# A macaron network on one core: first recurrence and mixer preparation, per sequence instead of per batch

## The chip, the core and the metric

The kernel runs on one core of a Trainium2 chip. A core has five engines that run side by side, each with its own queue, taken in order: TensorE (PE, matmuls and transposes, its weight loads listed as PEld), VectorE (DVE), ScalarE (ACT), GpSimd (POOL) and SyncE (SP, which here only issues transfers; ACT's queue issues a few as well). Matmul results land in PSUM, from where DVE and ACT fetch them. The metric is the device time of one execution in microseconds (us), lower is better; a matmul of 32-bit floats is two passes in the trace, each with a weight load.

## The reference, cut to what matters

Eight sequences of 512 tokens with 128 features go through four layers. Every layer is a half-weighted feed-forward part, a mixing part, and the same feed-forward part again, each on a layer-normed input and added to x. Only the first layer's first two parts are touched:

```python
def ffn(x, ...):                       # L0_ffn: a gated recurrence over the 8 SEQUENCES (the scan axis),
    def step(c, xt):                   # side by side for all 512 tokens
        ft = sigmoid(xt @ wf.T + c @ uf.T + bf)
        it = sigmoid(xt @ wi.T + c @ ui.T + bi)
        gt = tanh(xt @ wc.T + c @ uc.T + bc)
        return ft * c + it * gt, None
    c_final, _ = lax.scan(step, c0, x)
    return tanh(einsum('tbi,oi->tbo', x, wo) + c_final @ uo.T + bo)

def mixer(u, ...):                     # L0_attn: a state-space mixer along the tokens
    zxbcdt = u @ W_in.T                # z0, x0 (skip), xBC (conv), dt (8 heads)
    dt = softplus(dt + dt_bias); A = -exp(A_log)
    xBC = silu(causal_conv4(xBC) + conv_b)          # x, B, C
    h = exp(dt*A) * h + dt * x * B;  y = h . C + D * x        # step by step over the tokens
    y = layernorm(y) * ln_gamma + ln_beta
    y = sigmoid(y @ W_gate.T + b_gate) * y
    return concat([silu(z0) * x0, y]) @ W_out.T

x = x + 0.5 * ffn(layernorm(x)); x = x + mixer(layernorm(x)); x = x + 0.5 * ffn(layernorm(x)); ...
```

The outputs of the first part need c_final, so nothing of the mixer can begin before all eight steps of the recurrence are done.

## The kernel before

x stays on the chip all the way, one tile x0 to x7 per sequence (128 partitions, 4 chunks of 128 tokens, 128 features). The weights come in packs by one transfer each. The stages of the list `_STAGES` follow one another: l0_ffn, l0_attn, l0_ffn again, then the layers behind, which the diff does not touch. They take the span from about 495 us on.

The order in which Python emits the instructions is not quite the order on the engines. The framework's planner takes what is ready by its own estimate, earlier emitted first, when an engine is free; tiles with the same name in a pool share `bufs` buffers and are handed out in the order of emission. The result is a fixed order on each engine. The planner does not read the trace.

**l0_ffn** (L452) norms all sequences (`norm`, L331: statistics on DVE, power of -1/2 on POOL, application on DVE), turns them on PE to xT0 to xT7 (`transposed`, L434, copied from PSUM by ACT, L439), and runs the recurrence: for each sequence three gates, each a matmul with xT and one with c into a PSUM tile pf, pi or pc (L329 is the helper `mm`), an activation on ACT (L474), and on DVE fc, ig and the new c (L476 to L480). Behind the last step come the product of c with uo, the tile cb (L485), and for each sequence the product with wo, h (L491), its tanh (L492) and the half addition to x (`add_half`, L448).

**l0_attn** (L495) prepares the mixer for all eight sequences at once. `norms` (L360) takes four sequences together, with one power on POOL for 16 columns (L374), and applies on ACT (L381). After the first four, `mixer_in(0)` (L591) is emitted except its first piece: conv 2, 0, 1 (each a matmul, one ACT pass L609 and three DVE passes L612), skip 0 and 1 (L623, L624), silu (L630 to L633), and b_tokens (L660). Then for all 32 chunks together: 64 passes with w_dt, the softplus (L831 to L849, a power series in some 16 DVE instructions on 128x256, with one Exp on ACT), la = dt times the rates, three products with constant triangles (running sums), and from them cum, since_start, to_end and whole, kept in `self.tokens`.

The mixer's loop goes over the sequences; in a pass for b, pieces of five kinds are emitted by the slot numbers of `_MIXER`:

```python
_MIXER = dict(
    weights=(0, 4, 6, 12),
    sums=(9, 14, 21, 29),
    turned=(17, 23, 29, 35),
    inputs=(7, 19, 21, 23, 25, 27, 29, 31),
    out=(2, 6, 8, 10, 18, 22, 25),
)
```

`weights`, `sums` and `turned` are the four chunks of b (`chunk_weights` L675 with the Exp named decay, L702, read from the PSUM tile pr; `chunk_sums` L718 with brought and the state; `chunk_turned` L758); `inputs` is `mixer_in(b + 1)`, whose first piece, exponents, makes from cum the tiles from, to_rows and to (L646 to L652); `out` is `mixer_out(b - 1)` (L767: norm of y, turns, two sigmoid gates L804, product, addition to x L819). PSUM has three buffers of the name mm, three of ck, and one pr of two banks. The loop's pool sb has two buffers of a name unless it says otherwise.

A third way to norm stands further down and is used by later stages: `front` (L1175) gives two functions, stats (DVE statistics, POOL's power) and apply (an offset on DVE, four normalisations on ACT, L1200).

## Time and profile before

| | us |
|---|---|
| median of three runs | 2368.93 |
| the three runs | 2368.93, 2368.0, 2375.28 |
| span of the profiled execution (no time of its own is listed beside it) | 2372.5 |
| busy in the span: PE, DVE, ACT, POOL | 2109.1, 1631.6, 1269.6, 660.6 |
| c of the recurrence first multiplied, last c written | 27.6, 72.3 |
| first and second sequence's first decay | 151.45, 170.69 |
| mixer's last addition to x | 425.96 |
| TensorE clock granted, mean of the span | 0.937 |

A row of a group or of the timeline names the line, the engine, the operation and the tiles (out<-in). "[0.39 <-DVE c L466]" is the idle time of the engine before the instruction and what ended it. A row of busy times gives a stretch, its length, and the busy time of each engine in it with the number of instructions, then the granted TensorE clock (1.00 is full speed). The chain of waits is the chain of work that ended last, followed back from the end. Busy PE overlaps itself, since matmuls are pipelined.

### The profile page before, as it was taken

The page shows a single profiled execution, that of the slowest core. Times are in us where ns is not written, and L with a number is a line of the kernel's source. Part 1 is how long each engine was busy: PE and PEld are TensorE (multiplying, and loading weights), DVE is VectorE, ACT ScalarE, POOL GpSimd, SP SyncE. Part 2 cuts the span into 40 slices and gives each one's busy share as a digit, 9 for nine tenths or more (in the row PEclk, how much of TensorE's full clock was granted, in tenths as well). Part 3 has the DMA queues.
Part 4 walks back from the last instruction along what each step waited for, and adds up shares of the span by engine and source line. Part 5 has one row for each costly group of instructions (what it writes and reads, how often), then busy time and mean ns, then how long its engine had stood idle before and what let it go on. Part 6 is the DMA issues. An engine that isn't in the chain of part 4 may idle for free.

```text
span 2372.5 us, 30011 instructions
## 1 busy us (share of the span) xinstructions
PE 2109.1 (89%) x10967; PEld 1001.9 (42%) x10967; DVE 1631.6 (69%) x3830; ACT 1269.6 (54%) x1857; POOL 660.6 (28%) x923
## 2 busy tenths in 40 slices
PE   7679999979998888999996999896789999999989
PEld 3344444444433333333332444444445444444444
DVE  4556775368888788888827889888776556666611
ACT  3545665323322376777772446666674355555554
POOL 1124433013212011111113233446552123333330
PEclk9778998979999999999997999998897999999999
DMA  3000000000000000000000000000000000000001
GB/s 124 1 1 1 1 1 1 14 10 1 1 1 1 1 1 1 1 1 1 1 1 7 1 1 1 0 1 1 0 1 0 1 1 1 1 1 1 2 1 36
DMA packets 10035, 13.07 MB, mean 6 GB/s; under 512 B 416, under 2 KB 8736, under 8 KB 9760
## 3 DMA queue, kind: packets, MB, share of 16 engines
q1 hardware_dynamic: 7776, 10.11, 1.3%
q8 instruction: 86, 1.41, 0.3%
q10 hardware_dynamic: 2112, 1.05, 0.2%
q14 instruction: 61, 0.50, 0.1%
HBM read 9.06 MB, written 2.10 MB: 5 GB/s over the span
## 4 chain that ended last, share of the span: by engine, by line
PE 60%; DVE 23%; POOL 7%; ACT 7%; issue 3%; DMA 0%; ACTq 0%; DVEq 0%; SPq 0%; POOLq 0%
PE pair L329 11%; PE av L329 8%; PE mm L329 8%; PE po L329 6%; PE pu L329 5%; PE first L329 4%; DVE max L1673 4%; PE pg L329 3%; ACT e L1781 3%; PE ck L329 2%; PE pr L329 2%; DVE act L942 2%; PE big L329 1%; PE ph L329 1%; DVE xn L355 1%
## 5 line engine op out<-in xcount | busy, mean ns | idle before, releaser
L1673 DVE TENSOR_REDUCE max<-first 128x1 f32<-128x512 f32 (+3 forms) x756 | 468.3, 664 | 173.4 <-PE first L329 166.1
L1781 ACT ACTIVATE e<-pair 128x1024 f32<-128x1024 f32 (+3 forms) x512 | 436.5, 864 | 239.3 <-PE pair L329 227.1
L329 PE MATMUL first<-qkT 32*128 32x512 f32 (+3 forms) x896 | 267.9, 443 | 30.5 <-DVE max L1673 28.7
L329 PE MATMUL pair<-qkT 32*128 32x512 f32 (+3 forms) x1024 | 222.5, 454 | 20.0 <-ACT e L1781 14.6
L329 PE MATMUL av<-e,v 128*32 128x512 f32 (+3 forms) x2048 | 238.9, 536 | 0.1
L941 ACT ACTIVATE act<-pg 128x512 f32<-128x512 f32 x144 | 85.6, 596 | 212.9 <-PE po L329 122.0
L329 PEld LDWEIGHTS pair<-qkT 32*128 32x128 f32 x1024 | 95.2, 185 | 233.6 <-ACT e L1781 133.2
L329 PE MATMUL pair<-mT,max_rows 32*128 32x512 f32 (+3 forms) x1024 | 190.4, 374 | 1.7 <-DVE mT L1715 1.7
L329 PE MATMUL pu<-xT,w_moe 128*128 128x512 f32 x288 | 158.4, 632 | 18.8 <-DVE act L942 14.0
L1783 POOL TENSOR_SCALAR_AFFINE_SELECT e<-e 128x256 f32<-128x256 f32 x256 | 103.4, 407 | 253.4 <-ACT e L1781 253.1
L329 PE MATMUL po<-act,w_moe 128*128 128x512 f32 x288 | 161.3, 647 | 5.4 <-DVE act L949 4.2
L329 PE MATMUL pg<-xT,w_moe 128*128 128x512 f32 x288 | 150.5, 620 | 4.4 <-ACT act L941 3.3
L329 PEld LDWEIGHTS first<-qkT 32*128 32x128 f32 x896 | 119.6, 185 | 69.4 <-DVE max L1673 66.9
L942 DVE TENSOR_TENSOR act<-act,pu 128x512 f32<-128x512 f32 x144 | 97.8, 679 | 28.8 <-PE pu L329 23.5
L1679 POOL COPY copies<-max 128x128 f32<-128x128 f32 x64 | 23.6, 424 | 272.4 <-DVE max L1673 272.4
L329 PEld LDWEIGHTS pair<-mT,max_rows 32*128 32x128 f32 x1024 | 96.9, 188 | 3.0 <-DVE mT L1715 2.7
L1673 DVE TENSOR_REDUCE max<-mm 128x1 f32<-128x512 f32 (+3 forms) x108 | 70.9, 665 | 36.7 <-PE mm L329 35.5
L949 DVE TENSOR_TENSOR act<-act,big 128x512 f32<-128x512 f32 x128 | 86.3, 677 | 12.3 <-PE big L329 11.8
L329 PEld LDWEIGHTS pu<-xT,w_moe 128*128 128x128 f32 x288 | 50.2, 196 | 76.8 <-DVE act L942 37.0
L329 PEld LDWEIGHTS po<-act,w_moe 128*128 128x128 f32 x288 | 50.5, 199 | 63.5 <-issue 28.1
L978 POOL TENSOR_TENSOR ge<-ge,w_moe 128x64 f32<-128x64 f32 (+1 forms) x32 | 42.8, 1336 | 119.1 <-DVE ge L976 113.6
L329 PEld LDWEIGHTS pg<-xT,w_moe 128*128 128x128 f32 x288 | 51.1, 195 | 57.2 <-issue 40.1
(423 smaller groups left out, 4398.2 us busy)
## 6 DMA issues: line engine op xcount, KB each, us to landing
w_moe<-in_moe SPq DMA_DIRECT2D x1, 2392.0 KB, 14.0
out<-x SPq DMA_DIRECT2D x8, 256.0 KB, 2.3
x<-in_u ACTq DMA_DIRECT2D x4, 256.0 KB, 6.6
x<-in_u SPq DMA_DIRECT2D x4, 256.0 KB, 6.4
w_mixer<-in_l0a SPq DMA_DIRECT2D x1, 960.5 KB, 8.2
w_mixer<-in_l1a SPq DMA_DIRECT2D x1, 769.0 KB, 4.8
w_ffn<-in_l0f SPq DMA_DIRECT2D x1, 578.0 KB, 7.2
w_ffn<-in_l2f SPq DMA_DIRECT2D x1, 560.0 KB, 3.3
```

Of the source, the lines that this page charges most:

```text
L329: self.nc.tensor.matmul(out, lhsT, rhs, start=start, stop=stop)
L355: nc.vector.tensor_scalar(xn[:, c, :], x[:, c, :], mv[:, c, 0:1], rstd[:, c : c + 1], ALU.subtract, ALU.mult)
L941: nc.scalar.activation(act, pg, AF.Silu)
L942: nc.vector.tensor_tensor(act, act, pu, ALU.mult)
L949: nc.vector.tensor_tensor(act, act, pw[:, e % 2, :], ALU.mult)
L978: nc.gpsimd.tensor_tensor(ge.rearrange(flat), ge.rearrange(flat), self.wide(before, m), ALU.mult)
L1673: nc.vector.tensor_reduce(mx[:, c, j, gs[0] : gs[-1] + 1], sc, AX.X, ALU.max, negate=True)
L1679: nc.gpsimd.tensor_copy(copies[:, :, :, :, g], mx[:, :, :, g].unsqueeze(3).to_broadcast([P, NC, 4, 8]),)
L1781: nc.scalar.activation(e[:, :, :n], sc[:, :, :n], AF.Exp, scale=scale)
L1783: nc.gpsimd.affine_select(e[:, :, :P], e[:, :, :P], pattern=[[0, 2], [1, P]], compare_op=ALU.is_ge, fill=0.0, base=0, channel_multiplier=-1,)
```

## The change

The first l0_ffn leaves the list of stages; its recurrence moves into l0_attn as `l0_chain`, and its outputs go into a new list of six pieces per sequence, `mixer_ready`: out (product with wo, h, tanh, half addition), stats and apply (with `front`), turned, steps (w_dt, softplus, la) and sums (running sums and their exponentials). In `l0_chain` the norm and the turn of a sequence are emitted right before its own step of the recurrence, with statistics one sequence ahead. The pieces of sequences 0 and 1 are emitted ahead of the mixer's loop, mixed with `mixer_in(0)`; those of sequence b + 2 are emitted in the loop's pass for b, at the slots `ready`. What was one tile for all 32 chunks in `self.tokens` becomes a tile of 32 columns per sequence, with two buffers. The transfers at the start change their order: on SP x0, w_const, w_ffn, x2, x4, x6, then the other packs; on ACT x1, x3, x5, x7 as before.

```diff
@@ -222,6 +222,7 @@
     out=(2, 6, 8, 10, 18, 22, 25),
+    ready=(3, 5, 11, 13, 16, 24),
@@ -299,11 +300,19 @@
+        self.ident = None
+
+        def fetch(eng, b):
+            eng.dma_start(out=self.x[b], in_=u[b].rearrange("(c p) d -> p c d", p=P))
+
+        fetch(nc.sync, 0)
         self.load("const")
-        for b in range(NB):
-            eng = nc.sync if b % 2 == 0 else nc.scalar
-            eng.dma_start(out=self.x[b], in_=u[b].rearrange("(c p) d -> p c d", p=P))
-        for name in ("l0f", "l0a", "moe", "heads", "l2a", "l3f"):
+        for b in range(1, NB, 2):
+            fetch(nc.scalar, b)
+        self.load("l0f")
+        for b in range(2, NB, 2):
+            fetch(nc.sync, b)
+        for name in ("l0a", "moe", "heads", "l2a", "l3f"):
             self.load(name)
         self.ident = self.w["const", "ident"]
         self.nhalf = const.tile([P, 4 * NC], F32, name="nhalf")
@@ -492,82 +501,90 @@
+    def l0_chain(self, keep):
+
+
+        nc = self.nc
+        w = lambda n: self.w["l0f", n]
+        self.xT = [keep.tile([P, L], F32, name=f"xT{b}") for b in range(NB)]
+        self.last_c = keep.tile([P, L], F32, name="last_c")
+        with ExitStack() as s:
+            sb = s.enter_context(self.pool("sb", 2))
+            ps = s.enter_context(self.pool("ps", 2, space=bass.MemoryType.PSUM))
+            c = sb.tile([P, L], F32, name="c")
+            nc.vector.memset(c, 0.0)
+            nc.vector.tensor_scalar(c, c, w("in_c"), None, ALU.add)
+            fronts = [self.front(b, "i", 2, lambda: sb) for b in range(NB)]
+            for b in range(NB):
+                if b == 0:
+                    fronts[0][0]()
+                if b + 1 < NB:
+                    fronts[b + 1][0]()
+                fronts[b][1]()
+                self.transposed(fronts[b][2]["xn"], ps, self.xT[b], nc.scalar.copy)
+                gates = {}
+                for gate, func in (("f", AF.Sigmoid), ("i", AF.Sigmoid), ("c", AF.Tanh)):
+                    pg = ps.tile([P, L], F32, name=f"p{gate}")
+                    self.mm(pg, w("w" + gate), self.xT[b], stop=False)
+                    self.mm(pg, w("u" + gate), c, start=False)
+                    gates[gate] = sb.tile([P, L], F32, name=f"g{gate}")
+                    nc.scalar.activation(gates[gate], pg, func, bias=w("b" + gate))
+                fc = sb.tile([P, L], F32, name="fc")
+                nc.vector.tensor_tensor(fc, gates["f"], c, ALU.mult)
+                ig = sb.tile([P, L], F32, name="ig")
+                nc.vector.tensor_tensor(ig, gates["i"], gates["c"], ALU.mult)
+                c = sb.tile([P, L], F32, name="c") if b + 1 < NB else self.last_c
+                nc.vector.tensor_tensor(c, fc, ig, ALU.add)
+
     def l0_attn(self):
...
         with ExitStack() as s:
             keep = s.enter_context(self.pool("keep", 1))
+            self.l0_chain(keep)
             sb = s.enter_context(self.pool("sb", 2))
             ps = s.enter_context(self.pool("ps", 3, space=bass.MemoryType.PSUM))
             self.key, self.sb, self.ps = "l0a", sb, ps
-            for b in range(0, NB, 4):
-                for k, xn in enumerate(self.norms(range(b, b + 4), keep)):
-                    t = keep.tile([P, L], F32, name=f"xT{b + k}")
-                    xT.append(self.transposed(xn, ps, t, nc.scalar.copy))
-                if b == 0:
-                    self.seqs = [{"xT": xT[0]}]
-                    first = self.mixer_in(0)
-                    for piece in first[1:]:
-                        piece()
-            self.seqs += [{"xT": t} for t in xT[1:]]
-            pd = ps.tile([P, NB * NC, H], F32, name="mm")
...
-            nc.vector.tensor_tensor(v, pd, self.wide(w("dt_bias"), NB * NC), ALU.add)
-            dt = keep.tile([P, NB * NC, H], F32, name="dt")
-            self.softplus(dt.rearrange("p t h -> p (t h)"), v.rearrange("p t h -> p (t h)"), keep)
...
+            self.seqs = [{} for _ in range(NB)]
+            pc = ps.tile([P, NC, P], F32, name="mm")
+            for t in range(NC):
+                self.mm(pc[:, t, :], self.last_c[:, bass.ts(t, P)], self.w["l0f", "uo"])
+            self.cb = keep.tile([P, NC, P], F32, name="cb")
+            nc.vector.tensor_tensor(self.cb, pc, self.wide(self.w["l0f", "bo"]), ALU.add)
+            ready = [self.mixer_ready(b) for b in range(NB)]
+            a = self.rates = keep.tile([P, H], F32, name="a")
             nc.scalar.activation(a, w("A_log"), AF.Exp)
...
-            pcum = ps.tile([P, n], F32, name="mm")
-            self.mm(pcum, self.w["const", "upto"], la_flat)
...
-            since_start = keep.tile([P, n], F32, name="since_start")
-            nc.scalar.activation(since_start, pcum, AF.Exp)
...
-            self.tokens = dict(
-                dt=dt, cum=cum, since_start=since_start, to_end=to_end, whole=whole
-            )
+            self.ones16 = keep.tile([P, S], F32, name="ones")
+            nc.gpsimd.memset(self.ones16, 1.0)
+            for piece in ready[0][:4]:
+                piece()
+            first = self.mixer_in(0)
+            first[1]()
+            ready[0][4]()
+            ready[1][0]()
+            ready[0][5]()
+            first[0]()
             self.mask_ki = keep.tile([P, 4, P], BF16, name="mask_ki")
             nc.vector.tensor_scalar(
                 self.mask_ki, self.wide(self.w["const", "upto"]), -MASKED, MASKED, ALU.mult, ALU.add
             )
             self.ident16 = keep.tile([P, P], BF16, name="ident16")
             nc.vector.tensor_copy(self.ident16, self.ident)
-            first[0]()
+            first[2]()
+            first[3]()
+            first[6]()
+            ready[1][1]()
+            first[7]()
+            first[4]()
+            ready[1][2]()
+            first[5]()
+            for piece in ready[1][3:]:
+                piece()
...
                     turned=[lambda c=c: self.chunk_turned(b, c) for c in range(NC)],
+                    ready=ready[b + 2] if b + 2 < NB else [],
                 )
...
+    def mixer_ready(self, b):
...
+        q = self.seqs[b]
+        stats, apply, t = self.front(b, "e", 2, lambda: sb)
...
+        def out():
+            po = ps.tile([P, NC, P], F32, name="mm")
+            for c in range(NC):
+                self.mm(po[:, c, :], self.xT[b][:, bass.ts(c, P)], self.w["l0f", "wo"])
+            h = tile_("h", NC, P)
+            nc.vector.tensor_tensor(h, po, self.cb, ALU.add)
+            nc.scalar.activation(h, h, AF.Tanh)
+            self.add_half(b, h)
+
+        def turned():
+            q["xT"] = self.transposed(t["xn"], ps, self.xT[b], nc.scalar.copy)
+
+        def steps():
+            pd = ps.tile([P, NC, H], F32, name="mm")
+            for c in range(NC):
+                self.mm(pd[:, c, :], q["xT"][:, bass.ts(c, P)], w("w_dt"))
+            v = tile_("dt_in", NC, H)
+            nc.vector.tensor_tensor(v, pd, self.wide(w("dt_bias")), ALU.add)
+            q["dt"] = tile_("dt", NC, H)
+            self.softplus(flat(q["dt"]), flat(v), sb)
+            q["la"] = tile_("la", NC, H)
+            nc.vector.tensor_tensor(q["la"], q["dt"], self.wide(self.rates), ALU.mult)
+
+        def sums():
+            la = flat(q["la"])
+            p = ps.tile([P, 3, n], F32, name="mm")
+            self.mm(p[:, 0, :], self.w["const", "upto"], la)
+            self.mm(p[:, 1, :], self.w["const", "after"], la)
+            self.mm(p[:S, 2, :], self.ones16, la)
+            lead = sb.tile([P, n], F32R, name="cum_lead")
+            nc.vector.tensor_copy(lead, p[:, 0, :])
+            cum = q["cum"] = tile_("cum", NC, 2, 2, H)
+            by_tile = lambda ap: ap.rearrange("p (t h) -> p t h", h=H)
+            for k in range(2):
+                nc.gpsimd.tensor_copy(cum[:, :, k, 0, :], by_tile(lead.bitcast(F32)))
+                nc.vector.tensor_tensor(
+                    cum[:, :, k, 1, :], by_tile(p[:, 0, :]), by_tile(lead.bitcast(F32)), ALU.subtract
+                )
+            q["since_start"] = tile_("since_start", n)
+            nc.scalar.activation(q["since_start"], p[:, 0, :], AF.Exp)
+            q["to_end"] = tile_("to_end", n)
+            nc.scalar.activation(q["to_end"], p[:, 1, :], AF.Exp)
+            q["whole"] = tile_("whole", n, rows=S)
+            nc.scalar.activation(q["whole"], p[:S, 2, :], AF.Exp)
+            nc.vector.tensor_tensor(q["to_end"], q["to_end"], flat(q["dt"]), ALU.mult)
+
+        return [out, stats, apply, turned, steps, sums]
...
-                self.tokens["cum"][:, b * NC : (b + 1) * NC].rearrange("p t x y h -> p (t x y h)"),
+                q["cum"].rearrange("p t x y h -> p (t x y h)"),
...
-        nc.vector.tensor_tensor(heads(dtx), heads(px), per_head(tok["dt"][:, t, :]), ALU.mult)
+        nc.vector.tensor_tensor(heads(dtx), heads(px), per_head(q["dt"][:, c, :]), ALU.mult)
...
-                heads(brought), heads(pb), per_head(tok["since_start"][:, cols]), ALU.mult
+                heads(brought), heads(pb), per_head(q["since_start"][:, cols]), ALU.mult
...
 _STAGES = [
-    "l0_ffn",
     "l0_attn",
     "l0_ffn",
```

## Prediction

> **What bounds the kernel now.** I read the page first, then the chain of waits over the first 190 us, then the timeline there, and last the busy times by stretch in the mixer's steady part, because the diff touches only the first quarter of the span. The page's execution has a span of 2372.5 us; the runs have a median of 2368.93 (2368.0 to 2375.28). No separate time is listed for the profiled execution, so I work out a difference in its span (3.6 us above the median) and take it off the median. Some 0.3% (7 us) is what a measurement here can tell from no change.
>
> From the timeline (start, length, engine, line, instruction), the marks that the sum is made between:
>
> ```profile
> 27.60 1.13 PE L329 MATMUL pf<-c,w_ffn 128*128 128x512 f32 x2 [0.39 <-DVE c L466]
> ...
> 71.59 0.69 DVE L480 TENSOR_TENSOR c<-fc,ig 128x512 f32<-128x512 f32 x1
> ...
> 151.45 1.02 ACT L702 ACTIVATE decay<-pr 128x1024 f32<-128x1024 f32 x1 [1.28 <-PE pr L329]
> ...
> 170.69 1.02 ACT L702 ACTIVATE decay<-pr 128x1024 f32<-128x1024 f32 x1
> ```
>
> The gate recurrence starts at 27.6 and ends at 72.3; the first decay of sequence 0, where the mixer's loop really begins, comes at 151.45, and that of sequence 1 only 19.24 later. The 79 us between 72.3 and 151.45 are a serial chain. Its largest pieces (start, length), from the chain of waits:
>
> ```profile
> 72.34 4.52 PE mm L329 x24
> 92.14 2.94 POOL many_rstd L374
> 95.31 6.27 ACT xn L381 x16
> 110.52 6.70 PE mm L329 x8
> 121.81 11.87 PE mm L329 x64
> 135.40 1.76 DVE softplus_z L841
> 143.47 2.06 PE mm L329 x4
> ```
>
> Each is work for four or eight sequences at once that sequence 0 must sit through. The granted clock is 0.60 over 87 to 150 us.
>
> From decay to decay of sequences 2 to 7 the loop looks like this (stretch, length, then busy us of PE, PEld, DVE, ACT, POOL, and the clock):
>
> ```profile
> 208.93:245.60 36.67, 35.66 (x165) 15.23 (x163) 24.96 (x59) 22.18 (x31) 14.59 (x19) 0.86 0.00 0
> 245.60:279.56 33.96, 32.63 (x165) 14.41 (x163) 25.82 (x58) 22.18 (x32) 14.57 (x19) 0.95 0.00 1
> 279.56:313.52 33.96, 32.63 (x165) 14.56 (x163) 25.80 (x58) 22.18 (x31) 14.56 (x19) 0.95 0.01 1
> 313.52:346.89 33.37, 32.61 (x165) 14.58 (x163) 23.84 (x54) 22.18 (x32) 14.50 (x19) 0.95 0.00 1
> 346.89:379.47 32.58, 31.09 (x165) 13.97 (x163) 23.73 (x54) 22.18 (x31) 14.49 (x19) 1.00 0.00 1
> ```
>
> DVE has 8 to 10 us free in each, ACT 11, POOL 19. PE's 32 of 34 is pipelined overlap: its weight loads fill only 14.5. Yet over 245 to 280 us PE lines carry some 64% of the chain of waits (mm 33.3, ck 12.8, pr 10.7, the turns 6.6).
>
> **Earlier start.** w_const, first on SP's queue, landed 3.6 us after its issue at 0.79; x0 takes that place, so x0 is there at 4.4. w_ffn was issued at 5.65 behind four x and landed 7.2 later. Now only x0 and w_const are ahead on SP, with ACT's four x beside them; 2.1 MB at the 300 GB/s of that stretch is 7 us, so it lands near 9.5. x2, x4, x6 move behind w_ffn, w_mixer and the later packs one place back; their first users come after 15 us, so I cost that at nothing (2 us if x2 came late). After x0: stats 4 x 0.26, POOL's 0.23 and 1.04, offset 0.2, four ACT normalisations at 0.39, last turn and copy 0.9: 9.7. First c matmul at 10.5, against 27.6.
>
> **The chain itself** does not shrink. In steady state it issues a matmul pass every 0.43 us with 12 passes a step, 5.2 us, so PE sets it. Twelve of the 96 passes, and the turns of seven sequences, were done before 27.6; now all lie inside: 96 x 0.43 = 41.3, 32 turns at 0.12 = 4, the last c's trip through tanh and two products 2.5, and the half-clock patch of the last steps (pf 2.07 instead of 1.07) 1.6. Sum 49.4, plus 1 for a table load (1.28) if the early Exp of A_log falls in. It ends at 61 (56 to 66): gain 11.3.
>
> **From c to the first decay.** Only sequence 0 is served. From the rows: matmul, cb, h, tanh and add, 5.8 (72.30 to 78.17); stats 1.1, POOL 1.5, offset 0.2; four normalisations 1.6, turn and copy 0.9: 11.1. Conv 2 (matmul 1.1, ACT 0.78, three DVE passes at 0.73) puts the softplus at 15.2. For a softplus of 32 columns the trace has the same lines at 1 and at 256 columns (min/median/max ns):
>
> ```profile
> L846 DVE SCALAR_TENSOR_TENSOR softplus_acc<-softplus_acc,softplus_sq x14: 147/424/1856, 138.4 to 601.5; 128x256 f32<-128x256 f32 x7, 128x1 f32<-128x1 f32 x7
> L1049 DVE RECIPROCAL x_inv<-x_scale 128x32 f32<-128x32 f32 x16 | 5.3, 334 | 0.0
> ```
>
> Between 147 and 425 ns, 32 columns give 0.18. Twelve such, three scalar ones at 0.165 and the reciprocal of 0.334 are 3.0, with gaps 3.3; dt_in and la 0.4. The three running sums on PE 1.0, lead and POOL's copies 0.6, turn 0.35, the two scalings 0.8, POOL's "to" 1.9, pr 1.3: 25. The second sequence's outputs (1.4) and convs 0 and 1 (six at 0.73) share DVE, and one table load lies before Exp: I take 30 (24 to 36) where it was 79.2. First decay at 91 instead of 151.45: **gain 60.5**.
>
> **Given back in the first loop.** Its 19.24 us was short because three chunks' turns, x_tok, dtx and the skips stood ready. Now it is a whole period less the missing mixer_out (some 6 of 33.96), plus skip 0 (3): 31. **Loss 11.8.**
>
> **Given back in six loops.** Each of the loops 0 to 5 takes on a sequence's ready pieces. DVE: h and add 1.37, stats 1.04, offset 0.17, dt_in 0.2, softplus 3.3, la 0.18, four for the sums 0.8: 7.1 us. PE: outputs 8 passes 0.97, turns 0.45, w_dt 8 passes (11.87/64 = 0.185 at a clock of 0.57; nearer 0.12 at full) 1.0, sums 0.7: 3.1. ACT: tanh 0.63, normalisations 1.6, copy 0.58, four small Exp at 0.2: 3.6, and zero to three table loads at 1.28. POOL: 1.27 and two copies of 0.2. ACT's 7.5 at most and POOL's 1.7 fit into their idle 11 and 19, so I cost them at nothing; without that cover ACT would add up to 7.5.
>
> What DVE's share costs is bounded by two rows above with the same clock of 0.95: 33.96 with DVE 25.82 (it takes in the next stage's norms) and 33.37 with 23.84. So 0.59 us for 1.98 of DVE work, 0.30 each: 7.1 gives 2.1. PE's 3.1 counts between 64% and whole: 2.0 to 3.1. I take 4.6 a loop. The floor is 1, since denser PE work could also lift the clock (the loop took 36.67 at 0.86 and 32.58 at 1.00); the ceiling is 10.2, DVE and PE end to end. Six loops: **loss 27.6** (6 to 61).
>
> A wait is added here: the new since_start of sequence b+2 has two buffers and needs that of b, read last by chunk_sums(b, 3) at slot 29, while sums stands at 24. Its Exp waits on ACT, and p holds one of three "mm" banks meanwhile; behind it stand skip's matmuls. brought of the last chunk runs at 238.58 with conv 1's matmul at 236.68, so it is 1 to 3 us of one bank, inside the 4.6.
>
> Sum: -60.5 + 11.8 + 27.6 = -21.1: 2368.9 - 21.1 = **2348**. All later stages issue the same instructions, so nothing else moves. DVE is next: 25.8 + 7.1 of 38.6 us.
>
> **A rule against it.** In the trace a table load is 1.28 us and the next ACTIVATE follows at once (222.92 to 224.22), and ACT already loads four to six times a loop, since silu, exp and sigmoid alternate. The Trainium skill, ScalarE: Activation LUTs, says under "What ACT_TABLE_LOAD costs" that each switch takes about 2.66 us with its drain, and under "Table sets: the hidden batching unit" that work of one set should be done together; this change scatters tanh and exp over the loop. By 2.66 three more loads would be 8 us of ACT a loop, nearly all of its idle time, and up to 48 in all, as an estimate; by the row it is 3.8 and hidden. The same page puts tanh into exp's set too, which would spare two of the three; no row here shows an exp and a tanh without a load between.
>
> **Rivals.**
> *Cheaper loop.* The pieces fill gaps and the clock stays near 0.95 where loops 1 and 2 had 0.82 and 0.86; 2 us a loop gives -60.5 + 11.8 + 12 = -37: 2332. For it: ACT and DVE idle. Against: the chain of waits runs through PE. 0.25.
> *The loop eats it.* DVE's queue runs in order, and about 16 dependent softplus instructions stand in it ahead of decay products that PE waits for. At 10.2 a loop the sum is +12.5: 2381. It decides from 9.3 a loop on (gain gone and 7 us lost). For it: DVE would be the fullest engine. Against: the 0.30 row. 0.16.
> *The start gives little.* The chain ends at 66 because turns and normalisations push its sigmoids on ACT, and the start-up takes 36: gain 49.5, and with 6 a loop -1.7: 2367. 0.14.
>
> **How the numbers follow.** The forecast (2334 to 2361) has 0.45. Its own range with the cheaper loop below it and the other two above gives 2318 to 2376, leaving out 2 in 10. Faster by over 0.3% (under 2361.8) are the forecast and the cheaper loop, 0.70; within 0.3% the third rival, 0.14; slower 0.16.
>
> **What would show it.** In the changed profile: first c matmul near 10.5 (steps right if 9 to 13); last_c at 56 to 66; first decay of sequence 0 at 85 to 97; decay of sequence 1 some 31 later, not 19; decay periods of sequences 2 to 5 near 38.5, and of the last two, which carry no ready pieces, near 33 as before; DVE at 32 us in such a period. Wrong if the periods pass 43 with DVE or ACT full, if c starts after 16, or if the mixer's last addition to x (425.96 now) moves by less than 7 us.

## The result, and the profile after

The changed kernel takes 2405.15 us (median of 4 runs, 2398.14 to 2406.87) against 2368.47 us (4 runs, 2367.24 to 2375.28): ratio 1.0136, 95% interval 1.0109 to 1.0163. It is slower by 1.4%; the forecast was 2348, and even the rival "the loop eats it" had only 2381. The profiled execution has a span of 2404.6 us, 32.1 more than before.

The marks of the prediction, from the timeline of the changed kernel (start, length, engine, line, instruction), and below them the first and the last addition to x of the mixer in the kernel before:

```profile
16.40 1.06 PE L338 MATMUL pf<-c,w_ffn 128*128 128x512 f32 x1
66.15 0.69 DVE L537 TENSOR_TENSOR last_c<-fc,ig 128x512 f32<-128x512 f32 x1
99.30 1.02 ACT L779 ACTIVATE decay<-pr 128x1024 f32<-128x1024 f32 x1 [0.67 <-PE pr L338]
138.03 1.02 ACT L779 ACTIVATE decay<-pr 128x1024 f32<-128x1024 f32 x1 [3.98 <-PE pr L338]
198.95 0.69 DVE L896 TENSOR_TENSOR x<-x,mm 128x512 f32<-128x512 f32 x1 [0.39 <-PE mm L895]
458.24 0.69 DVE L896 TENSOR_TENSOR x<-x,mm 128x512 f32<-128x512 f32 x1 [12.52 <-PE mm L895]
```

```profile
201.20 0.69 DVE L819 TENSOR_TENSOR x<-x,mm 128x512 f32<-128x512 f32 x1
425.96 0.69 DVE L819 TENSOR_TENSOR x<-x,mm 128x512 f32<-128x512 f32 x1 [13.06 <-PE mm L818]
```

The first decay comes 52 us sooner (99.30, was 151.45). But the mixer's first addition to x comes at 198.95 where it was 201.20: 50 of the 52 us are gone within the first two passes. The last addition comes at 458.24 where it was 425.96, and these 32.3 us are the whole difference of the spans; nothing after the mixer moved (1946.4 us after, 1946.5 before).

I measure a pass from one addition to x to the next. The first four by stretch (length, then busy us of PE, PEld, DVE, ACT, POOL, and the clock), in the kernel before and in the changed one:

```profile
201.20:240.02 38.82, 37.81 (x184) 16.09 (x183) 26.21 (x61) 23.09 (x33) 15.32 (x20) 0.87 0.00 1
240.02:273.98 33.96, 32.63 (x164) 14.41 (x163) 25.81 (x59) 22.18 (x32) 14.57 (x19) 0.95 0.00 1
273.98:307.94 33.96, 32.63 (x164) 14.57 (x163) 25.80 (x58) 22.18 (x32) 14.56 (x19) 0.95 0.01 1
307.94:341.30 33.36, 32.60 (x164) 14.57 (x163) 23.83 (x54) 22.17 (x32) 14.50 (x19) 0.95 0.00 1
```

```profile
198.95:239.91 40.96, 37.83 (x199) 18.47 (x202) 33.92 (x92) 28.73 (x45) 15.99 (x23) 0.92 0.00 1
239.91:281.85 41.94, 38.98 (x199) 19.12 (x195) 32.35 (x93) 27.66 (x44) 17.27 (x24) 0.88 0.00 0
281.85:325.80 43.95, 40.54 (x196) 19.67 (x194) 31.79 (x92) 27.91 (x44) 16.70 (x24) 0.84 0.00 1
325.80:369.05 43.25, 40.76 (x196) 19.57 (x192) 30.44 (x88) 27.66 (x43) 16.04 (x23) 0.84 0.00 1
```

The first of the four is 2 us longer, the others 8 to 10, not 4.6. DVE (32) and ACT (28) are where I put them and neither is full; what I had not expected is the clock. Inside the third of these passes, in the same columns:

```profile
281.85:292.00 10.15, 9.77 (x55) 4.92 (x49) 9.37 (x31) 9.99 (x19) 2.35 (x5) 1.00 0.01 2
292.00:302.00 10.00, 7.11 (x53) 3.72 (x57) 9.78 (x23) 7.24 (x9) 7.45 (x11) 1.00 0.01 2
302.00:316.00 14.00, 13.86 (x57) 6.69 (x49) 6.14 (x22) 5.28 (x11) 4.57 (x6) 0.51 0.00 0
316.00:325.80 9.80, 9.80 (x40) 4.33 (x43) 6.50 (x19) 5.40 (x7) 2.34 (x4) 1.00 0.01 2
```

For ten us at the front DVE runs almost without a gap (9.78 of 10.00) and PE waits 2.9 us in all: 1.74 for POOL's wx, which stands in POOL's queue behind a norm that waits for DVE, 1.06 for a decay on DVE, 0.20 for a state. Then the clock is 0.51 for 14 us, in which PE is busy all the time. The chain of waits through that front (start, length, what), in part:

```profile
291.65 1.13 DVE decay L792
292.78 2.19 DVE y L364 x4
294.97 1.03 DVE x L457
...
296.33 1.13 DVE decay L792
...
299.26 1.04 POOL e_rstd L1268
300.30 0.68 POOL gated L882
...
301.49 1.91 POOL to L730
...
303.44 1.22 PE pr L338 x2
```

"x L457" and "e_rstd" are the ready pieces: they stand between the decays and ahead of "to", which the next exponents need.

### The profile page after: what moved, and what is told of

It is laid out like the page before. It is cut to its first block, busy times and chain, and to the rows that moved or that the text cites. A ratio compares the mean times of both kernels' runs of the same rounds, so it can differ in the third digit from the quotient of the medians.

```text
span 2404.6 us, 30322 instructions
## 1 busy us (share of the span) xinstructions
PE 2140.5 (89%) x11009; PEld 1013.7 (42%) x11009; DVE 1650.9 (69%) x3966; ACT 1297.9 (54%) x1928; POOL 669.5 (28%) x949
## 4 chain that ended last, share of the span: by engine, by line
PE 56%; DVE 22%; POOL 7%; ACT 7%; issue 3%; ACTq 0%; DVEq 0%; POOLq 0%
PE pair L338 11%; PE av L338 8%; PE mm L338 8%; PE po L338 6%; PE pu L338 5%; PE first L338 4%; DVE max L1750 4%; PE pg L338 3%; ACT e L1858 3%; PE ck L338 2%; DVE act L1019 2%; PE pr L338 1%; PE big L338 1%; PE ph L338 1%; DVE act L1026 1%
## 5 line engine op out<-in xcount | busy, mean ns | idle before, releaser
L1750 DVE TENSOR_REDUCE max<-mm 128x1 f32<-128x512 f32 (+3 forms) x108 | 71.0, 666 | 34.4 <-PE mm L338 33.6
```

The source lines that it names most:

```text
L1750: nc.vector.tensor_reduce(mx[:, c, j, gs[0] : gs[-1] + 1], sc, AX.X, ALU.max, negate=True)
```

## The experiments

Two theories. *Clock:* each pass has an idle front, the clock falls behind it, and the half-clock stretch is what makes a pass long. *Work:* a pass is a front set by DVE plus a rest set by PE; PE's and DVE's added work lies end to end in it, and the clock only follows. Rivals besides: table loads on ACT, the softplus series on DVE, the places of the pieces. Each run was timed beside the kernel before on the same chip; the ratios are to it (its medians were 2370.56 to 2375.42), the rows come from one execution each. With most edits the planner also orders some instructions anew.

**Parts of the change.** chain_only is the kernel before with the early recurrence and its order of loads alone:

```diff
-    # l0_ffn: eight norms and turns, then the recurrence
+    self.l0_chain(keep)          # as in the change; the rest as before
+    xT, c = self.xT, self.last_c
```

> The kernel before with the early recurrence alone (x0 first on SP's queue, weights of the recurrence second, normalisations and turns between the steps); outputs, norm, softplus and running sums stay batched over all sequences in front of the mixer's loop. All theories agree that the last c comes near 66.8 instead of 72.3 and that nothing else changes: 2363 (2360 to 2366). If the early chain itself does harm that I do not see (the clock after it, a table load), it is over 2369.

Ratio 1.0051 (1.0031 to 1.0072): slower. The start did gain: first decay 143.50, first addition to x 193.26, 8 us sooner. But the five passes after it take 39.1, 37.2, 37.3, 37.4 and 37.4 us where they took 38.8, 34.0, 34.0, 33.4 and 32.6:

```profile
232.37:269.59 37.22, 35.33 (x162) 15.00 (x163) 22.80 (x47) 22.19 (x32) 13.35 (x17) 0.86 0.00 1
```

The clock is 0.86 instead of 0.95. The record of the clock in the traces knows 0.5 and 1 only, and a stretch at 0.5 lasts 3.41 us or a whole multiple of it. In the kernel before the first of the five passes has three such steps, the next three one each and the last none; here each has three, and the four passes of the changed kernel shown above have two, three, four and four. With the clock held at 1.00 the same kernel has passes of 34.0 (chain_warm, below), so the steps are what makes these passes long.

Why three come here and not one is not shown. It need not be the earlier start, since the edit does more than was meant: `_STAGES` runs l0_ffn twice, and both are changed (the changed kernel keeps the old code for the second). The norms of the second one, which the kernel before does inside the mixer's loop, are gone from it (DVE 22.80 against 25.81), and PE takes some turns in another order. The second l0_ffn itself is longer, counted from the last addition to x of the mixer (425.96 and 431.88) to its own last one, in the kernel before and here:

```profile
493.67 0.69 DVE L448 SCALAR_TENSOR_TENSOR x<-h,x 128x512 f32<-128x512 f32 x1
```

```profile
505.46 0.69 DVE L456 SCALAR_TENSOR_TENSOR x<-h,x 128x512 f32<-128x512 f32 x1
```

So of the 19.1 us that this execution is longer, 5.9 are there at the end of the mixer, 5.9 come in the second l0_ffn (73.6 against 67.7), and 7.3 behind it, where nothing was changed; between all traces of this case that last part differs by up to 17 us (1869.1 to 1886.2). What holds is that the 8 us won at the start were lost again in five passes.

ready_ahead issues every sequence's pieces before the loop:

```diff
+            for b in range(2, NB): ready[b][0](); ready[b][1]()
+            for b in range(2, NB):
+                for piece in ready[b][2:]: piece()
-                    ready=ready[b + 2] if b + 2 < NB else [],
```

> The changed kernel with every sequence's outputs, norm, softplus and sums still in pieces for one sequence, but all of them issued before the mixer's loop. All theories of the loop say that its passes go back to 33 or 34 us from 42 to 44, so that from the third to the sixth addition to x the 31 us come back. What it tells is the price of the pieces outside the loop: with seven sequences' pieces at 7 us of DVE each the loop's start is some 50 us later than in the changed kernel for the second sequence: 2390 to 2410 if pieces are dear wherever they stand (unbatched work is the cost), under 2375 if it is their place in the loop that costs.

Ratio 1.0176 (1.0146 to 1.0206), 2417.78 and so above even the dearer forecast. The passes from the second on go back to 34.8, 36.4, 33.4, 32.6, but the second sequence's first decay is at 216.10 (138.03 in the changed kernel). In the 98 us from the first sequence's last decay to it the clock is 0.58, PE is busy for 53 and DVE for 60: one by one the pieces are dear outside the loop too.

late_ready moves the pieces behind the first decays:

```diff
-    ready=(3, 5, 11, 13, 16, 24),
+    ready=(13, 15, 19, 21, 24, 32),
```

> The changed kernel with the pieces for the sequence two ahead at places 13, 15, 19, 21, 24, 32 of a pass instead of 3, 5, 11, 13, 16, 24, so behind the decays of the first chunks. Queue theory: the addition to x (0.69), the stats (1.7) and POOL's two small operations at the front of the pass hold up the decays; behind them they cost 3 to 5 us less a pass, 2375 to 2390, and the clock's dip goes with them. If it is the sum of the work or the table loads, the place does not matter: 2400 to 2410.

Ratio 1.0097 (1.0080 to 1.0115); passes of 40.4, 45.1, 44.8, 42.9. Only the pieces' place changed, and a pass is not shorter: in the third, softplus steps stand ahead of la, for which PE waits 2.8 us, and POOL's e_rstd is in the chain of waits again. These other slots did not help; whether still others would, this one run cannot say.

**The clock held.** kept_warm adds PE work that nobody uses:

```diff
         pr = ps.tile([P, 2, 4, P], F32, name="pr", bufs=1)
+        for k in range(4 if c < 3 else 0):
+            self.mm(pr[:, k % 2], self.ident16, self.mask_ki)
```

> The changed kernel with four more 128x512 bf16 matmuls (mask by identity, into the bank that the real ones then overwrite) ahead of each of the first three chunks' decay exponents: work that nobody uses, 12 x 0.22 = 2.6 us of PE a pass. Clock theory: a pass loses 5 us because its front lets PE wait some 3 us and the granted clock then stays at 0.5 for 10 to 14 us; with PE kept busy the clock stays near 1 and a pass of 43 comes down to 38 or 39, 2375 to 2385 in all. Queue theory (DVE's and ACT's order is the bound, the clock only follows): a pass stays at 43 or takes the 2.6 us on top, 2405 to 2425.

Ratio 1.0026 (1.0008 to 1.0044): 1.1% faster than the changed kernel (1.0136), by adding work. The total is in the clock theory's range, but not by its way. The clock of the four passes rises from 0.92, 0.88, 0.84 and 0.84 to 0.96, 0.96, 0.92 and 1.00, yet they come down only to 40.9, 41.1, 42.7 and 41.3, 4.0 us in all; 6.6 us were won ahead of the first addition to x (192.40), 6.3 in the passes behind. The same matmuls in the kernel before (before_warm), and in it with sixteen more per pass (before_more_pe, `range((20, 4, 4, 0)[c])`):

> The kernel before with the same four unused 128x512 bf16 matmuls ahead of each of the first three chunks' exponents (12 x 0.22 = 2.6 us of PE a pass). Its passes have one half-clock stretch of 3.4 us each (clock 0.95) and the first two 5 to 10 us. If the dip is the price of an idle front, passes go from 34.0 to 32.6 or less and the first ones gain 2 or 3 each: 2360 (2356 to 2366). If the added work only takes its own time, 2369 to 2390.

> The kernel before with the unused matmuls and sixteen more of them ahead of each first chunk's exponents: 3.5 us of PE work a pass, about as much as the ready pieces bring, and nothing on DVE, ACT or POOL. In the kernel before with the first set a pass is 33.85 with PE busy 33.6. PE theory: one for one, passes of 37.3, 2360 + 7 x 3.5 = 2384. If there is still slack behind PE's busy share (its weight loads fill 14.8), 34.5 to 35.5, 2365 to 2371.

before_warm: 0.9950 (0.9933 to 0.9967), faster than before. before_more_pe: 1.0060 (1.0039 to 1.0080). One steady pass each of before_warm, before_more_pe and kept_warm, all at full clock:

```profile
265.55:299.40 33.85, 33.62 (x174) 14.83 (x175) 24.68 (x59) 22.08 (x32) 14.53 (x19) 1.00 0.00 1
```

```profile
238.25:275.37 37.12, 36.98 (x190) 16.42 (x191) 24.54 (x59) 22.19 (x32) 14.39 (x19) 1.00 0.00 1
```

```profile
317.16:358.51 41.35, 38.40 (x214) 18.68 (x217) 33.42 (x90) 27.26 (x44) 16.04 (x24) 1.00 0.01 1
```

At full clock, and with the twelve unused matmuls in it, the loop has no room on PE (33.62 of 33.85), and sixteen more, 3.5 us of PE and no work for another engine, lengthen it by 3.27: nearly one for one. That is shown. With the ready pieces a pass at full clock is 7.50 us longer: 4.78 more of busy PE and 2.72 more of PE waiting (2.95 against 0.23). So both theories hold a part, and work the larger one in these passes: 7.5 us is there without any dip. The higher clock shortened the changed kernel's passes by 0 to 1.9 us, with 2.6 us of added work in them.

**Which pieces.** On the base of kept_warm: without the first four pieces (warm_no_front), without the last two (warm_no_tail), without all six (warm_no_ready), each for sequences 2 to 7:

```diff
-                    ready=ready[b + 2] ...
+                    ready=[None] * 3 + [use_xT_as_it_is] + ready[b + 2][4:]   # warm_no_front
+                    ready=ready[b + 2][:4]      # warm_no_tail: values of sequence 1
+                                                # warm_no_ready: both
```

> The changed kernel with the unused matmuls, and without the first four pieces for sequences 2 to 7 (outputs of the recurrence, tanh, addition to x, norm and turn are left out; the mixer reads the turned input as the recurrence left it). Out of a pass of 41.2: DVE 2.6 at its front, PE 1.4, ACT 2.8, POOL 1.3. Front theory (a pass is the front, where DVE runs without a gap, plus the rest, where PE does): 4 us back, passes near 37, 2360 to 2366. If the tail pieces' table loads and softplus are the cost: 1 to 2 us back, 2370 to 2378.

> The changed kernel with the unused matmuls, and without the last two pieces for sequences 2 to 7 (their step sizes, softplus and running sums are left out; those of sequence 1 are used for all). Out of a pass of 41.2: DVE 4.5, PE 1.7, ACT 0.8 and two table loads of 1.28. Front theory: 2 to 3 us back (PE's share and little of DVE's), passes near 38.5, 2364 to 2370. Table or DVE-sum theory: 5 or more back, passes near 36, 2350 to 2358.

> The changed kernel with the unused matmuls and with no ready pieces for sequences 2 to 7 (their outputs of the recurrence, norm, turn, step sizes, softplus and sums are left out; they use the turned input as it is and the values of sequence 1). Passes should be 33.9 at a clock of 1.00, as in the kernel before with these matmuls. First addition to x: 192.4 with all pieces, 175 without the first four, 168 without the last two. If the pieces' costs add up, 151; if the pieces only fill time that lost preparation and the clock take anyway, 165. In all 2381 - 41 - 38 = 2302 for the first, 2318 for the second.

| | first addition to x | passes | last addition | median us |
|---|---|---|---|---|
| before_warm | 197.85 | 33.8, 33.9, 33.8, 33.8, 33.9 | 415.33 | 2360.19 |
| kept_warm | 192.40 | 40.9, 41.1, 42.7, 41.3, 34.6 | 441.40 | 2381.38 |
| warm_no_front | 175.29 | 39.1, 38.8, 40.7, 35.6, 34.7 | 412.37 | 2352.48 |
| warm_no_tail | 168.47 | 37.6, 37.4, 37.5, 35.6, 34.3 | 399.19 | 2342.89 |
| warm_no_ready | 165.70 | 34.1, 33.8, 33.9, 33.8, 33.8 | 383.83 | 2327.60 |

Each of these runs leaves work out, so its time is no kernel's. The first two came out lower than either of their forecasts, the third higher than both; the passes of 37.5 without the last two pieces lie between the 38.5 of the front theory and the 36 of the sums. Without pieces a pass is 33.85 again, with the instructions of before_warm's pass in the same order on PE. The pieces cost 57.6 us at the last addition (441.40 - 383.83): 26.7 of them ahead of the first addition, in two passes, the rest in the later ones. The two halves do not add up there: taking out either wins 17 or 24 of the 26.7. Both take away the same half-clock stretches: by the record of the clock there are 44 us of them from the first decay to the first addition with all pieces, 16 without the first four, 10 without the last two, 13 without any.

Which operations of the last two pieces? warm_no_loads turns their four exponentials into Identity, warm_no_series cuts the series:

```diff
-        nc.scalar.activation(e, e, AF.Exp, scale=-1.0)        # and three in sums
+        nc.scalar.activation(e, e, AF.Identity, scale=-0.01)  # warm_no_loads, b >= 2
-        for n in range(15, 1, -2):
+        for n in range(1, 1, -2):                             # warm_no_series, b >= 2
```

> The changed kernel with the unused matmuls; for sequences 2 to 7 the four small exponentials of the ready pieces are replaced by Identity (the exponentials are left out, their instructions stay), so that they ask for no table. A pass with ready pieces has 7 table loads (4 for 33.9 us passes without): table theory, two loads of 1.28 less and passes of 41.2 go down by 2.5 to 3, six passes 15 to 18 us, 2363 to 2367. Front-and-queue theory: ACT waits anyway, 0 to 1 us a pass, 2376 to 2384.

> The changed kernel with the unused matmuls; for sequences 2 to 7 the seven series steps of the softplus are left out (7 of some 50 small DVE instructions of a pass, 0.10 to 0.18 each). If DVE's sum were what a pass costs: 1 us less a pass. If what counts is that the series stands step by step between the convolution's passes, each waiting for the one before: 1 to 2 us less. If the tail's cost is ACT's or PE's: nothing. 2370 to 2380 for the first two, 2381 for the last.

warm_no_loads: the loads went from 7 to 5 a pass and the passes to 44 us at a clock of 0.92 (44.6, 44.3, 44.2, 44.0); 2393.64, not faster. warm_no_series: passes of 40.9, 43.8, 42.6, 43.8, 2385.07; a us less on DVE did not shorten them either. In both the first addition came sooner (183.98 and 185.60, against 192.40), and both have more half-clock steps in the passes than kept_warm and another order of instructions. So nothing was won by either, but a us or two a pass could be hidden by the clock (0.92 in the first, 0.88 to 0.96 in the second): that loads and series cost nothing is likely, not shown.

**PE's clock in the start-up.** start_warm puts four matmuls beside the softplus of sequence 0 of kept_warm; chain_warm2 (on chain_warm, below) has two behind each addition to x and ten beside the softplus:

```diff
+                for _ in range(4):                            # start_warm, in sums of b == 0
+                    self.mm(pw[: NC * H], flat(q["dt_in"]), self.xT[1])
+                    for _ in range(2):                        # chain_warm2, from the third addition to x on
+                        self.mm(pf, self.ident, self.x[b].rearrange("p c d -> p (c d)"))
```

> The changed kernel with the unused matmuls in the loop and four more 32x512 f32 ones while PE waits for the softplus of sequence 0 (0.5 of full clock from 74 to 98). The first two passes took 94 us from first decay to first addition to x, most of it at half clock (128 to 142, 146 to 162, 173 to 182). Clock theory of the first passes: the start of the loop comes 2 to 3 us sooner, and the dips move but do not go, since the waits at 124 to 128 and 140 to 148 are of DVE's softplus steps between the convolutions: 2376 to 2380. If these dips go as well: 2365 to 2372.

> The early recurrence with batched outputs, norm, softplus and sums, the unused matmuls in the loop, and more of them while PE waits in the start-up: two 128x512 f32 ones behind each sequence's addition to x from the third on, ten 128x256 f32 ones while the softplus runs. With the first set alone the clock was 0.5 from 82 to 100 and 115 to 140 and the first decay came at 144.9. Clock theory: turns, convolution and the step sizes' matmuls (some 20 us of PE at half clock) run at full clock, 5 to 8 us sooner: first decay at 137 to 140, 2354 (2350 to 2359). If the start-up is set by DVE, ACT and POOL and PE's clock does not matter: 2362, or more by what the added matmuls delay.

Both missed. start_warm: 2399.44; the first decay came 4 us later (102.11), with two matmuls of the convolution, 2.0 us, now between those for pr, and the dips only moved (first addition 203.66). chain_warm2: 2374.78, first decay 148.49 instead of 144.91. The clock was 1.00 over 76 to 88 us (0.69 in chain_warm), but there the unused matmuls stand in the chain of waits themselves:

```profile
76.54 5.15 PE warm L337 x12
```

The 64 matmuls of the step sizes start 3.8 us later for it (118.06, was 114.23), and over 120 to 132, where they are on the path, the clock stayed at 0.50. So neither run tells what a warm start-up would be worth. (The matmuls behind the additions are in the second l0_ffn too, which takes 81.8 us instead of 73.3; the total is no measure of the start-up.)

**Versions meant to win.** The early recurrence with all else batched, and the unused matmuls: twelve a pass (chain_warm); four, ahead of the second chunk alone (chain_light; before_light is the same without the early recurrence); four for sequence 0 and then twelve (chain_mixed) or eight (chain_mixed2):

```diff
+        for k in range(4 if c < 3 else 0):                      # chain_warm
+        for k in range(4 if c == 1 else 0):                     # chain_light, before_light
+        for k in range(4 if c == 1 or b and c < 3 else 0):      # chain_mixed
+        for k in range(4 if c == 1 or b and c < 2 else 0):      # chain_mixed2
```

> The early recurrence alone, as in the run before this one, with the same unused matmuls. There the start gained 8 us (first addition to x at 193.3 instead of 201.2) and five passes with the same instructions took 37.3 instead of 34.0, with a half-clock stretch of 10 us each instead of 3.4. Clock theory: the passes come down to 32.6 or less and the 8 us stay: 2352 (2346 to 2360), under both kernels. If something else in the early chain slows the passes, they stay at 37: 2385.

> The kernel before with four unused matmuls ahead of the second chunk's exponents alone (0.9 us of PE a pass instead of 2.6), where PE waits 0.7 us for y. If that stretch starts the dip, the clock stays at 1.00 and passes go to 32.2: 2350. If the other two sets were needed, the clock falls again to 0.95 and passes are 34: 2362 to 2369.

> The early recurrence with all else batched, and the four unused matmuls ahead of the second chunk's exponents alone. Without any, its first addition to x came at 193.3 (201.2 before) and its passes took 37.3. If the clock holds: passes 32.2, and the 8 us of the start stay: 2342. If it does not: passes 34 to 37, 2355 to 2385.

> The early recurrence with all else batched; unused matmuls as in the lighter set (four ahead of the second chunk's exponents) for sequence 0, and the full set of twelve from sequence 1 on. If the matmuls in the first pass were what pushed its first addition to x from 193 to 199: 193 + 5 x 33.9 + 30 + 18.2 = 411 for the last one (415.3 in the kernel before with the full set), 2352 to 2356. If the 8 us go wherever the matmuls stand: 2360 to 2364.

> The same with eight instead of twelve unused matmuls a pass from sequence 1 on (none ahead of the third chunk). PE theory: 0.8 us less a pass as long as the clock holds: passes of 33.0 and 407 for the last addition to x, 2348 to 2352. If the clock dips again: passes of 34 to 36, 2358 to 2370.

| | ratio to before | first addition | passes |
|---|---|---|---|
| chain_warm | 0.9957 (0.9937 to 0.9976) | 199.39 | 34.0 x5 |
| before_light | 0.9968 (0.9946 to 0.9991) | 199.22 | 34.4, 36.0, 33.2, 34.0, 34.1 |
| chain_light | 0.9972 (0.9952 to 0.9992) | 192.97 | 37.4, 33.5, 33.4, 34.4, 34.3 |
| chain_mixed | 0.9953 (0.9935 to 0.9970) | 193.19 | 34.0 x5 |
| chain_mixed2 | 0.9932 (0.9913 to 0.9951) | 187.80 | 35.5, 32.3 x4 |

chain_warm and chain_mixed2 fell between their forecasts, the other three met the less favourable one. chain_mixed2 has the lowest ratio of the complete kernels, 2355.35 us against 2372.27, and is faster than the kernel before and the changed one; its interval overlaps with that of before_warm (0.9950). What of it is the early recurrence stays open. At the last addition to x of the mixer chain_mixed is 3.4 us ahead of before_warm and chain_mixed2 16.0 (411.95, 399.30, 415.33), but their second l0_ffn, changed with the first, takes 73.7 and 73.2 us instead of 66.2, which gives back some 7. Neither the early recurrence in the first l0_ffn alone nor eight matmuls without it were run. A steady pass of it, where eight unused matmuls keep the clock at 1.00 and PE has no idle time left:

```profile
255.57:287.84 32.27, 32.25 (x172) 14.81 (x171) 22.58 (x45) 21.98 (x32) 13.35 (x18) 1.00 0.01 1
```

## Why the prediction was wrong

The forecast was -21.1 us at the end of the mixer; it was +32.3. The last additions to x divide it. The start with everything but the ready pieces: warm_no_ready against before_warm, 383.83 - 415.33 = -31.5. The pieces: +57.6. What the unused matmuls win, clock less their own work: 16.8 in the changed kernel (458.24 - 441.40) and 10.6 in the kernel before (425.96 - 415.33), so without them the two kernels lie 6.2 further apart. Sum +32.3. Against my terms the start gave 17.2 less than its 48.7, and the pieces, which I put at 27.6, cost 30.0 more. The price of the pieces in the loop is the step that failed most: I took PE's 32 of 34 for overlap with room in it, where at full clock there was next to none (31.1 of 32.6 in the last of my own rows), and I priced two cold passes like steady ones. The rows of these two passes, from first decay to first addition to x, in kept_warm and in warm_no_ready:

```profile
98.10:192.40 94.30, 83.46 (x363) 40.25 (x369) 55.50 (x162) 46.04 (x76) 26.36 (x40) 0.76 0.00 1
```

```profile
99.33:165.70 66.37, 63.87 (x323) 28.74 (x328) 44.03 (x100) 39.37 (x60) 23.15 (x32) 0.91 0.00 1
```

- *Earlier start and start-up:* gain 60.5 less 11.8, so 48.7, against 31.5. The direction was right. In the changed kernel itself the first decay gained 52.2, not 60.5: the first c matmul came at 16.4 instead of 10.5 (my sign of being wrong was 16; offset 0 stood on DVE, from 11.41, behind the statistics of two further sequences, whose x was there at 9.85, a wait that I had costed at nothing), the chain then took the predicted 50 and ended at 66.8, just past my upper end, and the start-up took 32.5 (I said 30). From first decay to first addition to x warm_no_ready takes 66.4 and before_warm 51.9: 14.5 lost, where I had 11.8.
- *First two passes' pieces:* 9.2 (two of six at 4.6) against 26.7. I costed the pieces at a steady loop's price, but these two passes run cold, at 0.76 with the pieces and 0.91 without (the rows above). At (1 - clock) x length, an estimate, 22.6 and 6.0 us are lost to the clock; 16.6 of the 27.9 us between them. The trace of before showed 0.60 over 87 to 150, and I read it only as the state of work that was to go.
- *Steady passes' pieces:* 4.6 against 7.5 at full clock, and 8 to 10 as run in three of four. PE was 4.8 instead of 3.1, and before_more_pe pays nearly one for one for PE's work. DVE's share by the 0.30 row (2.1) was near the 2.7 of waits, but that may be luck: the row came from the next stage's norms, while these pieces stand in a front where DVE has no gap. That denser PE work could lift the clock held for the unused matmuls alone; with the pieces it fell, from 0.95 to 0.84 to 0.92.
- *ACT and POOL at nothing:* no run speaks against it for the table loads; POOL's e_rstd stands in the chain of waits ahead of "to", so POOL's part need not be free; its price was not measured apart.
- *The rival* "the loop eats it" was right that the gain would go: three passes came near its 10.2. But they got there by PE's work, waits and the clock; that the softplus in DVE's queue did it is not borne out (warm_no_series won nothing, at another clock), and the total passed even its 2381. I gave it 0.16 because the row spoke for less.
- *The rule on tables.* I weighed the Trainium skill's page ScalarE: Activation LUTs, section "Table sets: the hidden batching unit". Its statement that exp and tanh share a set is now seen: h's tanh at 207.93, just after a decay's exp at 206.76, has no load of its own. Whether its advice to batch by set would have bought time is not shown here: two loads fewer a pass won nothing, at another clock.

What stays open: how a pass as run divides between work and clock. At full clock the pieces cost 7.5; multiplying the passes' length by their clock gives 32.3 for the passes of 33.96 before and 36.3 to 36.9 for the three of 42 to 44 after, so 4.0 to 4.6 of work and the rest clock. The two may differ because waits and half-clock stretches overlap; that is argued. Nor is it shown what starts the dips of the first two passes. The price of POOL's and DVE's waits was not measured apart, since the place of each piece also moves the dips.

## What to carry to other kernels

Before moving work from a serial start-up into a steady loop, ask which engine has room there at full clock, not in the averages: here PE had next to none, and 3.5 us of matmuls cost 3.3 us a pass, while much of the start-up is a chain through other engines. When a stage's code is used twice, an edit meant for one use changes the other. Where a loop's front makes PE wait, look at the granted clock in slices of 2 us; a few cheap matmuls that need no fresh data can be worth more than they cost. And a gain of a few us ahead of such a loop is proven only behind its last pass, since the steps of the clock in the loop can take it back.

## What the hardware showed

In the clock's record of all twenty traces the clock is 1 or 0.5, and every stretch at 0.5, but those with which a record ends, lasts 3.41 us or a whole multiple (one to four a pass in the loops above). The Trainium skill, TensorE: Matmul & The Clock Gate, Part 1, gives a free-running window of 3413 ns, and these steps agree. Its section on HAM oscillation states the rule as no idle gap above some 3.4 us; here the longest wait in the ten us ahead was 1.74 us, with PE busy 7.11 of 10.00, and the clock fell all the same. So no single long wait is needed; how little idle time is enough was not measured.

A PE that the profile shows as busy is not at full clock for that. In the pass shown above it is busy for 13.86 of 14.00 us at 0.51, and the matmuls of eight columns in the kernel before (128x8, 64 of them) fill PE and its weight loads end to end at 0.57. Whether their shape has a part in it, no run tells:

```profile
121.81:133.68 11.87, 11.86 (x64) 11.76 (x63) 0.00 (x0) 2.70 (x5) 1.77 (x3) 0.57 0.00 0
```
